# Row statistics of the FFN norm in a Mamba and FFN kernel: from VectorE's batch-norm instructions to ScalarE's accumulator output

## The chip, the cores and the metric

The kernel runs on one core of a Trainium2 chip. A core has five engines that run their own instruction streams and meet at semaphores: PE (TensorE, matrix products into PSUM), ACT (ScalarE, functions with a scale and a bias), DVE (VectorE, elementwise work and scans), POOL (GpSimd, elementwise work on SBUF) and SP (SyncE, which here issues all transfers). SBUF is the working memory with 128 partitions, PSUM holds the results of PE. The metric is the device time of one execution in microseconds (us); lower is better.

## The reference

The input `x` is 4 sequences of 2048 rows with 256 columns. One layer adds a Mamba block and then a feed-forward network (FFN), each behind a norm over the 256 columns of a row:

```
x = x + mamba(layernorm(x))        # mamba has its own norm, its own residual
x = x + ffn(layernorm(x))          # eps = 1e-5

def layernorm(x): m = mean(x, -1); v = var(x, -1); return (x - m) / sqrt(v + eps)

# mamba, inner width 512, 64 states for each inner channel:
xi, z = split(norm(x) @ W_in);  u = silu(causal_conv4(xi) + conv_b)
dt, B, C = split(u @ W_xproj);  delta = softplus(dt @ W_dt + b_dt)
h_t = h_(t-1) * exp(delta_t * A) + (delta_t * u_t) * B_t;   y_t = sum_n h_t * C_t
out = ((y + u * D) * silu(z)) @ W_out

# ffn, hidden width 768, int weights / 127:
ffn(x) = (silu(x @ wg.T) * (x @ wu.T)) @ wd.T
```

The change concerns the mean and variance of the second norm, the one ahead of the FFN.

## The kernel before

**Tiles and the scan.** The 4 x 2048 rows are worked off in 16 tiles of 512 rows (`NT = B * NQ`, tile number `n`). In a tile the recurrence over time is done as 256 scans on DVE (line 1472), each of 128 partitions by 512 time steps. Sixteen scans make a group; a group's data lie in one of three `ring` buffers. For one group, transfers spread the input `dusc` into the ring (`ring<-dusc`), POOL multiplies the ring by B in two instructions of eight scans each (line 1578), PE builds one bank of decay exponents for each scan in PSUM (line 1461, tile `a`, four banks), ACT takes their exponential in place (line 1467), DVE scans, and PE contracts the states with C (line 1496, evacuated by ACT at line 1517, and line 1530 with line 1539). After the last contraction of a group its ring is free for the next load. Line 1451 (POOL) and line 1482 (ACT) carry the state from one tile to the next.

**The dense work.** Everything else of a tile is done beside the scans of a neighbouring tile, in the order in which the main loop lists it. Beside the scans of tile `n` run: `front(n+1)` (first norm of the next tile, residual kept in the DRAM tensor `rsum`), `back(n-1)` (gate, output projection and residual of the tile before; result stored to `rsum`), `front_a(n+1)` and `front_b(n+1)` (projections, convolution, one `silu` on ACT with two table loads, softplus), and `back_b(n-1)` (second norm and FFN, with a `silu` and two table loads of its own). There are 15 such `back` and `back_b` pairs; the last tile has its own `back_early` and `back_last`.

**Residual and reload.** `residual` (line 1105) opens a PSUM bank, has ACT copy a half of the tile, 2 x 256 columns, into it (line 1112), lets PE add the products, and has ACT copy 512 columns back to SBUF (line 1115). `back` does this for both halves, then stores the tile to `rsum`. `back_b` loads it again, calls `layer_norm` and then `normalise` (line 520, four ACT instructions of 256 columns).

**The norm.** `layer_norm` (line 446) issues for each of four blocks of 128 rows a `bn_stats` and a `bn_aggr` on DVE (lines 469 and 470; mean and variance land in a PSUM bank `lp`). ACT then forms `var + eps`, its logarithm, `exp(-0.5 ln)` and a square (lines 479, 489, 490, 491), and three small DVE instructions (lines 494, 499, 504) refine the reciprocal root `rs` and form `nm = -mean * rs`.

**The order of the work.** A planner written in Python (`Planner.run`) lays out every engine's stream before the program is built. It simulates the engines with a cost for each operation and places, engine by engine, the operation with the smallest score. Scan work ("S") is scored by the time at which it could start. Dense work ("D") and contractions ("C") also have a due step, counted in scans; ahead of it they are scored up to 170 ns worse, behind it up to 230 ns better (`SLOPE`, `LEAD`, `LAG`). `dense` spreads the due steps of a tile's dense operations from step 8 to step 244 of its 256 scans, in proportion to the summed costs in program order. On PE and ACT dense work that would delay scan work by over 300 ns is scored another 300 ns worse (`HOLD`). Buffers of one name are handed out in program order. The kernel uses eight PSUM banks, four `a` and four `ps`; dense work takes its `ps` banks in program order and only where two are free. So a cost or an operation that is changed anywhere shifts due steps and can change the order elsewhere.

Of the kernel before, what the change touches and what calls it, by code (L numbers as in the profile page):

```python
# [15 lines left out]
AF = mybir.ActivationFunctionType  # L16
# [4 lines left out]
P = 128  # L21
T = 512
DM = 256
# [3 lines left out]
EPS = 1e-5  # L27
# [29 lines left out]
TINY = 60  # L57
SWITCH = 90
PAD = 0.0
SLACK = {"DVE": 300.0, "POOL": 300.0}  # L60


# [29 lines left out]
class Planner:  # L92
# [244 lines left out]
def mamba_ffn_kernel(  # L337
# [93 lines left out]
    def halves(t):  # L431
        return [(t, 0), (t, 1)]
# [11 lines left out]

        return t[:, b // 2, b % 2 : b % 2 + 2, :].rearrange("p a c -> p (a c)")

    def layer_norm(src, blocks=range(4), twice=False):

        nb = len(blocks)
        m = 2 if twice else 1
        lp, ve, rs, nm = buf("ps"), buf("s4"), buf("s4"), buf("s4")

        def sq():
            return lp.t[:, 16 : 16 + m * nb]

        def col(b):
            return b.t[:, 0 : m * nb]

        def mv():
            return lp.t[:, 0 : 2 * nb].rearrange("p (s c) -> p s c", c=2)

        def two(v):
            return v.rearrange("p (m s) -> p m s", m=m)

        def stats(j, s):
            st = buf("bst")
            op("DVE", 326, lambda: nc.vector.bn_stats(st.t, tok(src)[:, s, :]), [(src, s // 2)], [st])
            op("DVE", 205, lambda: nc.vector.bn_aggr(mv()[:, j, :], st.t), [st], [(lp, 0, j)])  # L470

        for j, s in enumerate(blocks):
            stats(j, s)
        mk = [(lp, 0, j) for j in range(nb)]

        def var(i):
            op(
                "ACT", 180,
                lambda: nc.scalar.activation(
                    ve.t[:, i * nb : (i + 1) * nb], mv()[:, :, 1], AF.Copy,  # L480
                    bias=EPS * EPS if i else EPS, scale=1.0 + EPS if i else 1.0,
                ),
                mk, [(ve, i)],
            )
# [17 lines left out]
        op(  # L502
            "DVE", TINY,
            lambda: nc.vector.scalar_tensor_tensor(  # L504
                two(nm.t[:, 0 : m * nb]), mv()[:, None, :, 0].to_broadcast([P, m, nb]), -1.0,
                two(rs.t[:, 0 : m * nb]), ALU.mult, ALU.mult,
            ),
            mk + [rs], [nm],
        )
        return rs, nm  # L510

    def normalise(dst, src, sc, blocks=range(4), o=0, ro=None):
        rs, nm = sc
        o -= blocks[0]
        ro = o if ro is None else ro

        def one(s):
            op(
                "ACT", act(DM, ptr=2),
                lambda: nc.scalar.activation(  # L520
                    tok(dst)[:, s, :], tok(src)[:, s, :], AF.Identity,
                    bias=nm.t[:, o + s : o + s + 1], scale=rs.t[:, ro + s : ro + s + 1],
                ),
                [(src, s // 2), rs, nm], [(dst, s // 2)],
            )

        for s in blocks:
            one(s)
# [176 lines left out]

    B2, yts, heads_in = {}, {}, {}

    rest, gates, last = {}, {}, {}

    def load_x(n):  # L710
        b, q = n // NQ, n % NQ
# [392 lines left out]
            ),  # L1104
        )

    def residual(pieces, reads, x1, h):

        ps = buf("ps")
        v = lambda: tok(x1)[:, h * 2 : h * 2 + 2, :].rearrange("p s c -> p (s c)")  # L1110
        open_bank(ps)
        op("ACT", act(), lambda: nc.scalar.copy(ps.t, v()), [(x1, h), ps], [ps])
        for cost, f in pieces:
            op("PE", cost, lambda f=f: f(ps.t), reads, [ps])
        op("ACT", act(T, True), lambda: nc.scalar.copy(v(), ps.t), [ps], [(x1, h)])

    def ev_add(x1, h):
        def ev(ps):
# [13 lines left out]
    def back(n):  # L1132
        r = n % R
        b, q = n // NQ, n % NQ
        y2 = buf("w8")
        for hf in range(2):
            for rh in range(2):
                ld = [buf(("yl", "w2")[rh]) for _ in range(2)]
                for _ in gate_y(n, y2, hf, rh, ld):
                    pass  # L1140
        x1 = buf("w4")
        load(lambda: tok(x1), rsum[r], 524288, r=[("rsum", r)], w=[(x1, 0), (x1, 1)])

        for h in range(2):
            yk = [(y2, hf, h) for hf in range(2)]
            residual(
                [mm_tok_add(wout, lambda k: y2.t[:, k, :], s, k, range(4)) for s in (2 * h, 2 * h + 1) for k in range(4)],
                yk + ["wout"], x1, h,
            )
        store(rsum[r], lambda: tok(x1), 524288, halves(x1), [("rsum", r)])  # L1150

    def back_b(n):
        r = n % R
        b, q = n // NQ, n % NQ
        x1 = buf("w4")
        load(lambda: tok(x1), rsum[r], 524288, r=[("rsum", r)], w=halves(x1))
        sc = layer_norm(x1)
        xn = buf("w4")
        normalise(xn, x1, sc)
        xT = buf("w4")  # L1160

        def ev_t(c):
            def ev(ps):
                op("ACT", act(T, True), lambda: nc.scalar.copy(xT.t[:, c, :], ps.t), [ps], [(xT, c)])

            return ev

        for c in range(2):
            transposes(xn, c, ev_t(c))
        hma, hmb = buf("w8"), buf("w4")  # L1170

        def hm(k):
            return hma.t[:, k, :] if k < 4 else hmb.t[:, k - 4, :]

        hk = [(hma, k) for k in range(4)] + [(hmb, k) for k in range(2)]

        def ev_g(k):
            def ev(ps):
                op("ACT", act(T, True), lambda: nc.scalar.copy(hm(k), ps.t), [ps], [hk[k]])

            return ev

        def ev_u(k):
            def ev(ps):
                up = buf("w2")
                op("ACT", act(T, True), lambda: nc.scalar.copy(up.t, ps.t), [ps], [up])  # L1186
                op(
                    "POOL", 1230, lambda: nc.gpsimd.tensor_tensor(hm(k), hm(k), up.t, ALU.mult),  # L1188
                    [up, hk[k]], [hk[k]],
                )  # L1190

            return ev

        for k in range(6):
            project(wgu, k * P, xT, ev_g(k), [("wgu", 0, k)])

        def silu():
            nc.scalar.activation(hma.t, hma.t, AF.Silu)
            nc.scalar.activation(hmb.t, hmb.t, AF.Silu)
            nc.scalar.preload_act_table_set(EXP_LN)  # L1200

        op("ACT", 5450, silu, hk, hk).tail = -1283.0
# [448 lines left out]
```

## Time and profile before

| quantity | value |
|---|---|
| median of 3 runs | 5000.17 us (4996.33 to 5005.06) |
| profiled execution, its own time | 4990.98 us |
| its span from first to last instruction | 4989.2 us |
| granted TensorE clock | 0.98 of full speed |
| DVE busy | 4758.8 us (95%) |
| POOL busy | 4697.7 us (94%) |
| PE busy | 4475.7 us (90%) |
| ACT busy | 3973.4 us (80%) |
| one tile, from its first scan to the next one's (tile 2) | 306.4 us: DVE 295.5, POOL 294.6, ACT 249.1 busy |

The profiled execution lies 9.2 us below the median of the timed runs. Busy shares are means over the whole span; an engine that is busy 95% of the time may still do a given instruction in a moment in which nothing else waits for it. The table tells how much work an engine has, not what that work is worth. For that one looks at which wait ends last around it: in the timeline of an engine the number in brackets is the time it sat idle before an instruction, and the arrow names what ended it.

### The profile page before, as it was taken

The numbers are of one execution on the slowest core, as the hardware profiler recorded it, in microseconds if no ns is written. First come the engines' busy times: TensorE is split into PE (matmuls) and PEld (weight loads), VectorE is DVE, ScalarE is ACT, GpSimd is POOL, SyncE is SP. The second block draws the span as 40 slices with busy tenths as digits, with TensorE's granted clock in tenths as the row PEclk, the third lists the DMA queues.
The fourth block names the chain that finished last, engine by engine and source line by source line (L and its number), as shares of the span: only waits on it lengthen the run. The fifth ranks groups of instructions, "written<-read, shape, count | busy, mean of one in ns | idle before, by whom it ended". The sixth has DMA issues, their size and how long they took to land.

```text
span 4989.2 us, 115894 instructions
## 1 busy us (share of the span) xinstructions
PE 4475.7 (90%) x46955; PEld 2171.1 (44%) x46955; DVE 4758.8 (95%) x4696; ACT 3973.4 (80%) x7138; POOL 4697.7 (94%) x862
## 2 busy tenths in 40 slices
PE   7889899899988989989998989989999898899888
PEld 2434344444444444444443434434444343444435
DVE  7999999999999999999999999999999999999996
ACT  6778878788787887878878787887878878788674
POOL 6999999999999999999999999999999999999994
PEclk9999999999999999999999999999999999999999
DMA  8676676666676767767667666667767677676762
GB/s 291 236 280 269 262 281 262 259 271 254 263 289 255 273 235 271 296 260 272 250 267 278 259 253 251 271 270 273 268 261 276 234 271 290 243 277 246 266 252 85
DMA packets 306346, 1299.86 MB, mean 261 GB/s; under 512 B 33617, under 2 KB 134737, under 8 KB 174866
## 3 DMA queue, kind: packets, MB, share of 16 engines
q1 hardware_dynamic: 305810, 1292.44, 67.3%
q8 instruction: 369, 6.05, 0.5%
q14 instruction: 167, 1.37, 0.1%
HBM read 1186.94 MB, written 105.38 MB: 259 GB/s over the span
## 4 chain that ended last, share of the span: by engine, by line
PE 41%; DVE 20%; ACT 15%; issue 10%; DMA 8%; POOL 5%; DVEq 0%; SPq 0%; POOLq 0%; ACTq 0%
DVE ring L1472 19%; PE a L1461 11%; PE ps L1496 9%; ACT a L1467 7%; PE ps L545 7%; DMA ring<-dusc 4%; PE ps L1097 4%; POOL ring L1578 4%; PE ps L779 3%; DMA yl<-qd 2%; PE ps L1530 2%; PE ps L898 2%; ACT mm L1517 1%; DMA dusc<-w 1%; PE ps L846 1%
## 5 line engine op out<-in xcount | busy, mean ns | idle before, releaser
L1578 POOL TENSOR_TENSOR ring<-ring,b 128x4088 f32<-128x4088 f32 (+2 forms) x512 | 4545.0, 8920 | 177.0 <-DMA ring<-dusc 110.3
L1472 DVE TENSOR_TENSOR_SCAN ring<-a,ring 128x512 f32<-128x512 f32 x4096 | 4595.0, 1195 | 104.9 <-ACT a L1467 62.5
L1467 ACT ACTIVATE a<-a,a 128x512 f32<-128x512 f32 x4096 | 2697.0, 665 | 707.3 <-PE a L1461 678.0
L1461 PE MATMUL a<-stk,selb 128*128 128x512 bf16 x5119 | 1806.7, 388 | 417.0 <-DVE ring L1472 376.5
L1496 PE MATMUL ps<-ring,cz 128*32 128x128 f32 x32768 | 1288.6, 279 | 11.1 <-issue 6.6
L1496 PEld LDWEIGHTS ps<-ring,cz 128*32 128x32 f32 x32768 | 786.3, 109 | 756.1 <-issue 699.2
L1461 PEld LDWEIGHTS <-selb 128*128 128x128 bf16 x5119 | 474.5, 98 | 1302.5 <-issue 1223.8
L545 PE MATMUL ps<-w,wgu 128*128 128x512 f32 x720 | 378.1, 608 | 0.0
L1517 ACT COPY mm<-ps 128x512 f32<-128x512 f32 x512 | 303.7, 593 | 53.0 <-PE ps L1496 52.0
L1530 PE MATMUL ps<-mm,exs 128*32 128x128 f32 (+1 forms) x4112 | 285.5, 407 | 5.8 <-ACT mm L1517 5.7
L545 PE MATMUL ps<-w,win 128*128 128x512 f32 x512 | 264.4, 601 | 0.3 <-ACT w L744 0.3
L779 PE MATMUL ps<-xi,w 128*128 128x512 f32 x480 | 248.6, 599 | 0.0
L1530 PEld LDWEIGHTS ps<-mm,exs 128*32 128x32 f32 x4112 | 117.3, 119 | 185.6 <-ACT a L1467 82.8
L1097 PE MATMUL ps<-wd,w 128*128 128x256 f32 x720 | 195.2, 387 | 0.0
L545 PEld LDWEIGHTS ps<-w,wgu 128*128 128x128 f32 x720 | 138.5, 194 | 103.9 <-issue 50.3
L1097 PEld LDWEIGHTS ps<-wd,w 128*128 128x128 f32 x720 | 132.5, 190 | 39.1 <-issue 12.7
L898 PE MATMUL ps<-w,ident 128*128 128x512 f32 x248 | 132.7, 618 | 2.8 <-ACT w L878 1.2
L1188 POOL TENSOR_TENSOR w<-w,w 128x512 f32<-128x512 f32 x90 | 114.6, 1301 | 16.0 <-ACT w L1186 15.8
L1097 PE MATMUL ps<-wout,w 128*128 128x256 f32 x480 | 128.8, 383 | 0.0
L545 PEld LDWEIGHTS ps<-w,win 128*128 128x128 f32 x512 | 96.6, 192 | 71.9 <-issue 48.8
L1041 PE MATMUL ps<-prm,yt 128*128 128x128 f32 x512 | 83.7, 294 | 34.6 <-ACT ps L1054 34.0
L520 ACT ACTIVATE w<-w,s,s 128x256 f32<-128x256 f32 x192 | 112.2, 592 | 1.9 <-DVE s L504 0.9
(147 smaller groups left out, 2381.9 us busy)
## 6 DMA issues: line engine op xcount, KB each, us to landing
ring<-dusc SPq DMA_DIRECT2D x1023, 1024.0 KB, 8.3
stk<-dsc SPq DMA_DIRECT2D x256, 96.0 KB, 5.5
qd<-w SPq DMA_DIRECT2D x32, 512.0 KB, 5.6
szd<-w SPq DMA_DIRECT2D x32, 512.0 KB, 8.3
dusc<-w SPq DMA_DIRECT2D x63, 256.0 KB, 3.6
dsc<-pk SPq DMA_DIRECT2D x63, 256.0 KB, 3.0
rsum<-w SPq DMA_DIRECT2D x31, 512.0 KB, 3.4
w<-rsum SPq DMA_DIRECT2D x31, 512.0 KB, 7.9
```

The source lines that it names most:

```text
L545: lambda ps: nc.tensor.matmul(ps, w[:, c, o : o + P], xT.t[:, c, :], start=(c == 0), stop=(c == 1)),
L779: lambda: nc.tensor.matmul(ps.t, dg.t[:, j * P : (j + 1) * P], xi.t[:, j : j + T], start=(j == 0), stop=(j == 3)),
L898: lambda: nc.tensor.matmul(ps.t, m, t.t, start=False, stop=True, skip_group_check=True),
L1097: lambda ps: nc.tensor.matmul(ps[:, (s % 2) * DM : (s % 2 + 1) * DM], src(k)[:, s * P : (s + 1) * P], w[:, k, :], start=False, stop=(k == ...
L1188: "POOL", 1230, lambda: nc.gpsimd.tensor_tensor(hm(k), hm(k), up.t, ALU.mult),
L1461: "PE", 216, lambda: nc.tensor.matmul(a.t, selb[:, p, :], stk.t, start=True, stop=True),
L1467: lambda: nc.scalar.activation(a.t, a.t, AF.Exp, scale=a2f[:, idx : idx + 1]), [a, "a2"], [a],
L1472: nc.vector.tensor_tensor_scan(v, a.t, v, 0.0, ALU.mult, ALU.add)
L1496: nc.tensor.matmul(pm.t[cg * 32 : cg * 32 + 32, (r8 % 4) * P : (r8 % 4 + 1) * P], framed(cz, blk), ring.t[:, :, blk * 8 : blk * 8 + 8], st ...
L1517: nc.scalar.copy(mm.t[:, hb * 4 : hb * 4 + 4].rearrange("p r a t -> p (r a t)"), pm.t)
L1530: nc.tensor.matmul(ex.t[jh * 32 : jh * 32 + 32, a * 16 : b * 16], framed(exs, jh * 2 + jl), mm.t[:, a:b, :, jh * 2 + jl], start=(jl == 0), ...
L1578: e.tensor_tensor(v, v, b2.t[:, None, t0:].to_broadcast([P, m, T - t0]), ALU.mult)
```

## The change

`residual` gets a tile `sums`. Where `back` calls it, the one copy of 512 columns out of PSUM becomes two ACT copies of 256 columns, each with an accumulator output that adds up its row. `back` then calls `layer_norm(x1, sums=sums)` itself, behind the store to `rsum`. In this form the norm has no `bn_stats` and `bn_aggr`: one ACT instruction makes minus the mean out of the four sums, and four ACT instructions of 256 columns square `x - mean` (the bias is minus the mean) into the upper half of the `lp` bank and add up the row. The variance is that sum over 256. The rest of the norm (lines 479 to 504) stays and moves along from `back_b` to `back`. `back_b` loads the tile as before and normalises it with the `rs` and `nm` that `back` left. `front`, and `back_last` of the last tile, keep the DVE form. A function `sums_of` is added but not called.

```diff
+ACC = 60.0
 ...
-    def layer_norm(src, blocks=range(4), twice=False):
+    def layer_norm(src, blocks=range(4), twice=False, sums=None):
 ...
+        def spread(s):
+            op(
+                "ACT", act(DM, ptr=1) + ACC,
+                lambda: nc.scalar.activation(
+                    lp.t[:, DM : 2 * DM], tok(src)[:, s, :], AF.Square,
+                    bias=sums.t[:, 4 + s : 5 + s], accum_out=sq4.t[:, s : s + 1],
+                ),
+                [(src, s // 2), (sums, 4)], [(lp, 2), (sq4, s)],
+            )
+
+        if sums is None:
+            for j, s in enumerate(blocks):
+                stats(j, s)
+            mk = [(lp, 0, j) for j in range(nb)]
+        else:
+            op(
+                "ACT", 180,
+                lambda: nc.scalar.activation(sums.t[:, 4:8], sums.t[:, 0:4], AF.Copy, scale=-1.0 / DM),
+                [(sums, s) for s in range(4)], [(sums, 4)],
+            )
+            for s in range(4):
+                spread(s)
+            mk = [(sq4, s) for s in range(4)]
 ...
-    def residual(pieces, reads, x1, h):
+    def residual(pieces, reads, x1, h, sums=None):
 ...
-        op("ACT", act(T, True), lambda: nc.scalar.copy(v(), ps.t), [ps], [(x1, h)])
+        if sums is None:
+            op("ACT", act(T, True), lambda: nc.scalar.copy(v(), ps.t), [ps], [(x1, h)])
+            return
+
+        def one(i):
+            s = h * 2 + i
+            op(
+                "ACT", act(DM, True) + ACC,
+                lambda: nc.scalar.activation(
+                    tok(x1)[:, s, :], ps.t[:, i * DM : (i + 1) * DM], AF.Copy, accum_out=sums.t[:, s : s + 1]
+                ),
+                [ps], [(x1, h), (sums, s)],
+            )
+
+        for i in range(2):
+            one(i)
 ...
         store(rsum[r], lambda: tok(x1), 524288, halves(x1), [("rsum", r)])
+        norms[n] = layer_norm(x1, sums=sums)
 ...
         load(lambda: tok(x1), rsum[r], 524288, r=[("rsum", r)], w=halves(x1))
-        sc = layer_norm(x1)
         xn = buf("w4")
-        normalise(xn, x1, sc)
+        normalise(xn, x1, norms[n])
```

More of the change, by code (lines that the diff above doesn't have):

```diff
@@ L445, in framed, with sums_of, one @@
         return t[:, b // 2, b % 2 : b % 2 + 2, :].rearrange("p a c -> p (a c)")
-    def layer_norm(src, blocks=range(4), twice=False):
+    def sums_of(src):
+        sums = buf("s4")
+        sink = buf("ps")
+        def one(s):
+            op(
+                "ACT", act(DM) + ACC,
+                lambda: nc.scalar.activation(
+                    sink.t[:, 0:DM], tok(src)[:, s, :], AF.Copy, accum_out=sums.t[:, s : s + 1]
+                ),
+                [(src, s // 2)], [sink, (sums, s)],
+            )
+        for s in range(4):
+            one(s)
+        return sums
+    def layer_norm(src, blocks=range(4), twice=False, sums=None):
         nb = len(blocks)
         m = 2 if twice else 1
-        lp, ve, rs, nm = buf("ps"), buf("s4"), buf("s4"), buf("s4")
+        lp = buf("ps")
+        sq4 = buf("s4") if sums else None
+        ve, rs, nm = buf("s4"), buf("s4"), buf("s4")
         def sq():
@@ L470, in stats, with var_in, minus_mean @@
             op("DVE", 205, lambda: nc.vector.bn_aggr(mv()[:, j, :], st.t), [st], [(lp, 0, j)])
-        for j, s in enumerate(blocks):
-            stats(j, s)
-        mk = [(lp, 0, j) for j in range(nb)]
+        def spread(s):
[17 more added lines that the diff above has]
+            )
+            for s in range(4):
+                spread(s)
+            mk = [(sq4, s) for s in range(4)]
+        def var_in():
+            return mv()[:, :, 1] if sums is None else sq4.t[:, 0:4]
+        def minus_mean():
+            return mv()[:, None, :, 0] if sums is None else sums.t[:, None, 4:8]
         def var(i):
@@ L479, in var @@
                 lambda: nc.scalar.activation(
-                    ve.t[:, i * nb : (i + 1) * nb], mv()[:, :, 1], AF.Copy,
-                    bias=EPS * EPS if i else EPS, scale=1.0 + EPS if i else 1.0,
+                    ve.t[:, i * nb : (i + 1) * nb], var_in(), AF.Copy,
+                    bias=EPS * EPS if i else EPS, scale=(1.0 + EPS if i else 1.0) / (1 if sums is None else DM),
                 ),
@@ L504, in layer_norm @@
             lambda: nc.vector.scalar_tensor_tensor(
-                two(nm.t[:, 0 : m * nb]), mv()[:, None, :, 0].to_broadcast([P, m, nb]), -1.0,
+                two(nm.t[:, 0 : m * nb]), minus_mean().to_broadcast([P, m, nb]), 1.0 if sums else -1.0,
                 two(rs.t[:, 0 : m * nb]), ALU.mult, ALU.mult,
             ),
-            mk + [rs], [nm],
+            (mk if sums is None else [(sums, 4)]) + [rs], [nm],
         )
@@ L706, in mamba_ffn_kernel @@
     B2, yts, heads_in = {}, {}, {}
-    rest, gates, last = {}, {}, {}
+    rest, gates, norms, last = {}, {}, {}, {}
     def load_x(n):
@@ L1114, in residual @@
             op("PE", cost, lambda f=f: f(ps.t), reads, [ps])
-        op("ACT", act(T, True), lambda: nc.scalar.copy(v(), ps.t), [ps], [(x1, h)])
+        if sums is None:
[3 more added lines that the diff above has]
+            s = h * 2 + i
+            op(
+                "ACT", act(DM, True) + ACC,
+                lambda: nc.scalar.activation(
+                    tok(x1)[:, s, :], ps.t[:, i * DM : (i + 1) * DM], AF.Copy, accum_out=sums.t[:, s : s + 1]
+                ),
+                [ps], [(x1, h), (sums, s)],
+            )
+        for i in range(2):
+            one(i)
     def ev_add(x1, h):
@@ L1142, in back @@
         load(lambda: tok(x1), rsum[r], 524288, r=[("rsum", r)], w=[(x1, 0), (x1, 1)])
+        sums = buf("s4")
         for h in range(2):
@@ L1147, in back @@
                 [mm_tok_add(wout, lambda k: y2.t[:, k, :], s, k, range(4)) for s in (2 * h, 2 * h + 1) for k in range(4)],
-                yk + ["wout"], x1, h,
+                yk + ["wout"], x1, h, sums,
             )
         store(rsum[r], lambda: tok(x1), 524288, halves(x1), [("rsum", r)])
+        norms[n] = layer_norm(x1, sums=sums)
     def back_b(n):
```

## The prediction

> **What bounds the kernel now.** I read the page first. DVE and POOL are both nearly full:
>
> ```profile
> PE 4475.7 (90%) x46955; PEld 2171.1 (44%) x46955; DVE 4758.8 (95%) x4696; ACT 3973.4 (80%) x7138; POOL 4697.7 (94%) x862
> ```
>
> Next, DVE's groups by shape. The scans make up 4595 us. The statistics instructions are 128 each, of which the change removes 60 (15 tiles x 4):
>
> ```profile
> L1472 DVE TENSOR_TENSOR_SCAN ring<-a,ring 128x512 f32<-128x512 f32 x4096 | 4595.0, 1195 | 104.9 <-ACT a L1467 62.5 <-POOL ring L1451 34.5 <-POOL ring L1578 7.7
> L469 DVE BATCH_NORM_STATS2 bst<-w 128x6 f32<-128x256 f32 x128 | 45.1, 410 | 26.6 <-DMA w<-rsum 24.8 <-DMA w<-in 1.7
> ...
> L470 DVE BATCH_NORM_AGGREGATE ps<-bst 128x2 f32<-128x6 f32 x128 | 21.8, 170 | 1.3
> ```
>
> This looks like a lot to win, so the third view asks where these instructions stand. DVE's timeline in tile 2, whose first scan starts at 667.8 us:
>
> ```profile
> 779.10 11.22 DVE L1472 TENSOR_TENSOR_SCAN ring<-a,ring 128x512 f32<-128x512 f32 x10
> 792.34 1.41 DVE L469 BATCH_NORM_STATS2 bst<-w 128x6 f32<-128x256 f32 x4 [2.02 <-DMA w<-rsum]
> 794.77 20.17 DVE L1472 TENSOR_TENSOR_SCAN ring<-a,ring 128x512 f32<-128x512 f32 x18 [1.02 <-ACT a L1467]
> ```
>
> All four bn_stats stand in one hole, between the scan that ends at 790.32 and the scan that starts at 794.77. What ends the hole is ACT: behind the bn_stats DVE waits another 1.02 us for an exponential. ACT's timeline says why:
>
> ```profile
> 787.49 1.28 ACT L947 ACT_TABLE_LOAD   x1
> 788.78 1.91 ACT L947 ACTIVATE w<-w 128x2048 f32<-128x2048 f32 x1
> 790.60 1.99 ACT L949 ACTIVATE w<-w 128x1024 f32<-128x1024 f32 x2
> 792.61 1.28 ACT L950 ACT_TABLE_LOAD   x1
> 793.90 0.27 ACT L1539 COPY yt<-ps 128x128 f32<-128x128 f32 x1
> 794.07 3.05 ACT L1467 ACTIVATE a<-a,a 128x512 f32<-128x512 f32 x5
> ```
>
> The silu of `front_b` holds ACT for 6.4 us (787.49 to 793.89), longer than the four banks of finished exponentials last (4 x 1.12 us). Tiles 1 to 14 all show it: the bn_stats of `back_b` stand 123.5 to 126.2 us into the tile, in a hole of 4.2 to 5.2 us, and the scan behind them waits 0.7 to 2.1 us for ACT. The hole is as long without them.
>
> Last, the waits of DVE and of POOL:
>
> ```profile
> DVE ring L1472 <- ACT a L1467: 62.5, 36, 3.5
> DVE ring L1472 <- POOL ring L1451: 34.5, 23, 5.4
> DVE bst L469 <- DMA w<-rsum: 24.8, 14, 3.1
> ```
>
> ```profile
> POOL ring L1578 <- DMA ring<-dusc: 110.3, 47, 31.1
> ...
> POOL w L1188 <- ACT w L1186: 15.8, 9, 3.0
> ```
>
> Each of the two waits for the other: POOL for a ring that the scans have left, DVE, some 286 us into most tiles, for POOL behind the FFN's six multiplications (line 1188). POOL alone has 294.6 us of work in a tile of 306.4.
>
> **Removed from DVE.** bn_stats in the holes of tiles 1 to 14: 56 x 0.35 us, and 24.8 us of waiting for the reload. Worth nothing on the path, as ACT ends the hole; were the silu gone it would be 19.7 + 24.8 = 44.5 us. In tile 15 (no `front_b`, no silu) the four stand between scans and lengthen the scan step by 0.31 us each: 1.25 us. bn_aggr: they stand about 207 us into the tile, among scans that follow each other at 1.115 us, and overlap with them; start to start, a lone one adds 0.07 us and a pair 0.29. Tiles 1 to 14 together 6.6 us (0.43, in two of them 0.74), tile 15 0.3. Sum: 6.6 + 0.3 + 1.25 = 8.2 us.
>
> The Trainium skill, "Perfetto Trace Analysis", section Identifying the Most-Contended Engine, has the engine with the highest occupancy worked on first and takes occupancy as a fair measure for Vector. By that rule the whole DVE time would count, 60 x (0.41 + 0.17) = 34.8 us, against 8.2 by the timeline. I go by the timeline.
>
> **Added to ACT.** Rows for it:
>
> ```profile
> L1115 ACT COPY w<-ps 128x512 f32<-128x512 f32 x60 | 35.3, 589 | 6.7 <-PE ps L1097 6.7
> ...
> L1054 ACT ACTIVATE ps<-w,dd 128x256 f32<-128x256 f32 x64 | 30.3, 484 | 4.4 <-PE ps L1078 4.1
> ...
> L1277 ACT COPY w<-ps 128x256 f32<-128x256 f32 x12 | 4.0, 371 | 2.3 <-PE ps L1294 2.3
> ```
>
> Copies: 4 x 0.371 for 2 x 0.589, +0.31 us. Minus the mean: 0.17 to 0.21 (lines 479 and 489). Squares: 4 x 0.484 = 1.94 (line 1054 also reads 256 columns with a pointer operand and writes PSUM). What an accumulator output costs stands in no row: at least 0, as more work cannot make the instruction shorter; at most a small ACT instruction of its own, 0.25 (line 911). I take 0.2 (lines 479 to 491 move 4 columns in 0.17 to 0.21): 8 x 0.2 = 1.6 (0 to 2.0). Sum 4.05 us a tile, 61 us in all (36 to 67). It is hidden: between 717 and 735 us, where `back` ends, ACT is busy 13.65 of 18 us and idles 0.2 to 0.45 us before nearly every exponential for want of a free bank; four banks of lead cover a run of such pieces. Without that cover it would cost its 61 us.
>
> The Trainium skill, "ScalarE: Activation LUTs", section Rules for kernel authors, speaks against the move: adds and multiplications belong on VectorE, up to about 3x faster per element in bf16. The rows here, fp32, have 0.410 for a bn_stats against 0.484 for the nearest ACT form, 1.2x. By 3x a Square would be 1.23 us, 45 us more on ACT in all.
>
> **Moved.** (a) The load of `rsum` stays; what waits for it is no longer DVE but `normalise` on ACT. In tile 2 it lands during the silu, so 0 us; at most DVE's 24.8 us, passed on to ACT, with the exponentials queued behind. (b) On SP the store of `back` waits for four copies instead of two, about 0.3 + 4 x 0.2 = 1.1 us longer, with ring loads queued behind it. In tile 2 it was issued at 730.68 and the next load still had to wait for its own ring until 736.8; in tiles 1 to 5 that wait is 5.2 to 7.6 us. 0 us; without that cover 15 x 1.1 = 16. (c) The bank `lp` is now held at the end of `back`, ahead of `front_a`, until the small DVE instructions come due (step 57 by my sum of the planner's costs, 68 us; `back` ends at 57 to 63). `front_a` works with one bank fewer for up to 10 us. It has slack: `dsc` is done at about 205 us and wanted by ring loads from about 250 (three groups of 18 us ahead of the tile's end). 0 us; at most 5 us a tile, and the waits would be on `a` and the next tile's loads.
>
> (d) `back_b` loses its only DVE instructions. Its bn_aggr came due at step 173 of 256, 206 us, and that is where they ran (206 to 210). PE's dense products pause for it from 867.8 to 886.3 us in tile 2. Without that chain (aggregates 874, `normalise` 881 to 885) the FFN can start up to 14 us earlier, ahead of its due steps, where the planner's score no longer pushes it before scan work. POOL's waits for the up-projection's copies are 15.8 us; DVE's for POOL behind them are larger (34.5 + 7.7). Between all of the 15.8 won and as much lost, as the order there is new; I take half won, 7.9 us, because early work is scored behind POOL's multiplications.
>
> Sum: 4990.98 - 8.2 - 7.9 = 4974.9 for a profiled execution. The median of the runs lies 9.2 us above the profiled one, so 4984.
>
> **Rivals.** *It is all hidden.* POOL is the bound when the bn_aggr go: lead of POOL over DVE is 0 to 1 us at each tile's start, so 8 us less on DVE is waited for POOL. Result 4992 to 5000. For it: POOL's 94%. Against it: POOL idles 2 to 4 us some 250 us into most tiles for a ring, after the bn_aggr.
>
> *It pays in full.* 34.8 + 24.8 us, 4940. Against it: the hole ends by ACT in all 14 tiles. It needs the planner to lay the silu otherwise.
>
> *Slower: `normalise` goes in right behind the silu.* Its statistics are ready early now, its input lands during the silu, and a bank for its output is free then. Four instructions of 0.59 us, 2.37 us, would stand where ACT has no lead left, and scans wait for them: 15 x 2.37 = 35.5 us, less 8.2, so 5027. It decides from 0.55 us a tile (8.2 / 15), and is measurable from 1.2. For it: the scans wait for ACT at this place already, and in tiles 9 and 13 again 30 us later (3.5 and 2.0). Against it: the planner scores exponentials first, and the dense copies that stand there now cost no wait.
>
> **How the numbers follow.** 0.2%, 10 us, is about what a measurement of this kernel can tell from no change. Forecast, a gain of 10 to 35 us: 0.34, own range 4965 to 4990. Hidden: 0.28. In full: 0.06. Slower: 0.32; as the planner lays out every stream anew, the same kind of wait may come up in another place, and no row excludes it. Faster 0.34 + 0.06 = 0.40. The range runs from 4950, half of the full gain's cases, to 5040, the slow rival with 13 us to spare; it leaves out about 0.15.
>
> **What would show it.** Right: line 469 falls from 128 to 68 instructions, the hole 125 us into a tile stays at 4 to 5 us with nothing in it and ends by ACT; the FFN's transposes come some 14 us earlier; POOL's wait at line 1188 falls; ACT's busy time rises by 36 to 67 us. Wrong: the hole shrinks with the bn_stats (full gain), or DVE's 62.5 us of waiting for line 1467 rise by over 10 us behind the silu (slower), or DVE's waits for POOL take up all that was saved.

## The result and the profile after

The changed kernel takes 5167.14 us (median of four runs, 5160.06 to 5241.46) against 4999.86 us for the kernel before on the same chip: a ratio of 1.0332 (95% interval 1.0317 to 1.0346). It is 3.3% slower. The forecast was 4984 with a range of 4950 to 5040; the result lies 127 us above that range. The execution profiled first was the longest of the four (5241.46 us) and is left out of the ratio as a slow run, so the same kernel was profiled a second time (5168.25 us, close to the median); the lines here are from that second profile. Line numbers from here on are those of the changed kernel: the scan is L1535, its exponential L1530, POOL's multiplication L1641, the last small instruction of the norm L551 (L504 before), `normalise` L567.

The busy line of the changed kernel. DVE is at 95% as before, but of a span that is 177 us longer, and its busy time is 144 us more although 120 instructions left it:

```profile
PE 4507.0 (87%) x46869; PEld 2175.0 (42%) x46869; DVE 4902.4 (95%) x4576; ACT 4002.5 (77%) x7363; POOL 4695.3 (91%) x862
```

DVE's groups by shape (busy time, mean ns of one, idle time before them and what ended it) say which instruction that is:

```profile
L1535 DVE TENSOR_TENSOR_SCAN ring<-a,ring 128x512 f32<-128x512 f32 x4096 | 4593.3, 1191 | 145.4 <-ACT a L1530 85.2 <-issue 51.2 <-POOL ring L1514 4.5
L551 DVE SCALAR_TENSOR_TENSOR s<-s,s 128x4 f32<-128x4 f32 x15 | 172.3, 11487 | 0.0
...
L490 DVE BATCH_NORM_STATS2 bst<-w 128x6 f32<-128x256 f32 x68 | 23.7, 400 | 0.1
...
L491 DVE BATCH_NORM_AGGREGATE ps<-bst 128x2 f32<-128x6 f32 x68 | 11.3, 167 | 0.7
```

The scans are as they were and the 60 + 60 statistics instructions are gone. But the instruction that forms `nm = -mean * rs` on four columns now takes 11.5 us on average, fifteen times: 172.3 us. This execution is 172.5 us longer than the median of the kernel before beside it (4995.79). That the two agree so closely is chance, as an experiment below shows: without these stalls the time falls by 150 us, and another loss is left.

Before the change the same instruction, line 504, read:

```profile
L504 DVE SCALAR_TENSOR_TENSOR s<-ps,s 128x4 f32<-128x4 f32 x15 | 2.0, 133 | 0.0
```

The same line is used by the first norm and by the last tile's norm, where nothing was changed. The view of that one source line in the changed kernel (minimum/median/maximum of the duration in ns, first and last start) puts the two side by side:

```profile
L551 DVE SCALAR_TENSOR_TENSOR s<-ps,s x18: 128/138/166, 7.7 to 5131.8; 128x8 f32<-128x8 f32 x16, 128x2 f32<-128x2 f32 x2
L551 DVE SCALAR_TENSOR_TENSOR s<-s,s x15: 136/9410/25477, 436.6 to 4909.0; 128x4 f32<-128x4 f32 x15
```

With twice the columns and one operand in PSUM (`ps`) it takes 0.14 us; with both operands in SBUF (`s,s`) it takes anything from 0.14 to 25.5 us. The operand that moved is minus the mean. The description of the change says that lines 479 to 504 stay; line 504 does, but its input does not. The diff says so in lines that the excerpt above leaves out (shortened):

```diff
+        def minus_mean():
+            return mv()[:, None, :, 0] if sums is None else sums.t[:, None, 4:8]
...
-                two(nm.t[:, 0 : m * nb]), mv()[:, None, :, 0].to_broadcast([P, m, nb]), -1.0,
+                two(nm.t[:, 0 : m * nb]), minus_mean().to_broadcast([P, m, nb]), 1.0 if sums else -1.0,
```

`mv()` is a view of the bank `lp` in PSUM, `sums` is a tile in SBUF. What the instruction waits for shows in the timelines of DVE and of POOL around one of them, in tile 4:

```profile
1374.51 1.21 DVE L1535 TENSOR_TENSOR_SCAN ring<-a,ring 128x512 f32<-128x512 f32 x1
1375.64 23.93 DVE L551 SCALAR_TENSOR_TENSOR s<-s,s 128x4 f32<-128x4 f32 x1
1399.49 8.07 DVE L1535 TENSOR_TENSOR_SCAN ring<-a,ring 128x512 f32<-128x512 f32 x7
```

```profile
1337.72 61.82 POOL L1641 TENSOR_TENSOR ring<-ring,b 128x4096 f32<-128x4096 f32 x7
1427.06 8.93 POOL L1641 TENSOR_TENSOR ring<-ring,b 128x4096 f32<-128x4096 f32 x1 [27.51 <-PE ps L826]
```

POOL multiplies without a pause from 1337.72 to 1399.54. The small instruction starts at 1375.64 and ends at 1399.57, with POOL's last multiplication. DVE works in order, so no scan runs in these 24 us. POOL, which needs the rings that the scans leave, then stands idle for 27.5 us. Its waits have grown accordingly (waits of POOL: total us, times, longest; the first was 110.3 us before):

```profile
POOL ring L1641 <- DMA ring<-dusc: 164.2, 47, 31.3
POOL ring L1641 <- PE ps L826: 62.2, 3, 27.5
POOL ring L1641 <- PE a L1524: 56.7, 12, 17.9
```

The six tiles in which L551 takes 15 us or more last 318 to 332 us, the three in which it takes less than 1 us 305 to 307.

### The profile page after: what moved, and what is told of

Same layout as the page of the kernel before. It is cut to its first block, busy times and chain, and to the rows that moved or that the text cites. A ratio compares the mean times of both kernels' runs of the same rounds, so it can differ in the third digit from the quotient of the medians.

```text
span 5239.7 us, 115514 instructions
## 1 busy us (share of the span) xinstructions
PE 4462.2 (85%) x46554; PEld 2171.1 (41%) x46869; DVE 4975.7 (95%) x4576; ACT 4002.9 (76%) x7363; POOL 4694.6 (90%) x862
## 5 line engine op out<-in xcount | busy, mean ns | idle before, releaser
L1641 POOL TENSOR_TENSOR ring<-ring,b 128x4088 f32<-128x4088 f32 (+2 forms) x512 | 4537.7, 8891 | 418.2 <-DMA ring<-dusc 217.9
L1535 DVE TENSOR_TENSOR_SCAN ring<-a,ring 128x512 f32<-128x512 f32 x4096 | 4594.7, 1197 | 147.4 <-ACT a L1530 86.8
L1530 ACT ACTIVATE a<-a,a 128x512 f32<-128x512 f32 x4096 | 2704.5, 665 | 911.6 <-PE a L1524 852.3
L1524 PE MATMUL a<-stk,selb 128*128 128x512 bf16 x4729 | 1729.0, 390 | 641.9 <-DVE ring L1535 609.3
L1559 PE MATMUL ps<-ring,cz 128*32 128x128 f32 x32768 | 1302.3, 280 | 28.9 <-issue 4.3
L1580 ACT COPY mm<-ps 128x512 f32<-128x512 f32 x512 | 304.2, 594 | 15.8 <-PE ps L1559 15.1
L826 PE MATMUL ps<-xi,w 128*128 128x512 f32 x480 | 268.9, 644 | 2.4 <-ACT ctail L821 2.3
L551 DVE SCALAR_TENSOR_TENSOR s<-s,s 128x4 f32<-128x4 f32 x15 | 245.3, 16353 | 0.0
L826 PEld LDWEIGHTS ps<-xi,w 128*128 128x128 f32 x480 | 95.1, 205 | 302.4 <-issue 286.6
## 6 DMA issues: line engine op xcount, KB each, us to landing
szd<-w SPq DMA_DIRECT2D x32, 512.0 KB, 11.5
```

The costliest lines, as they stand in the source:

```text
L551: lambda: nc.vector.scalar_tensor_tensor(two(nm.t[:, 0 : m * nb]), minus_mean().to_broadcast([P, m, nb]), 1.0 if sums else -1.0, two(rs.t[ ...
L826: lambda: nc.tensor.matmul(ps.t, dg.t[:, j * P : (j + 1) * P], xi.t[:, j : j + T], start=(j == 0), stop=(j == 3)),
L1524: "PE", 216, lambda: nc.tensor.matmul(a.t, selb[:, p, :], stk.t, start=True, stop=True),
L1530: lambda: nc.scalar.activation(a.t, a.t, AF.Exp, scale=a2f[:, idx : idx + 1]), [a, "a2"], [a],
L1535: nc.vector.tensor_tensor_scan(v, a.t, v, 0.0, ALU.mult, ALU.add)
L1559: nc.tensor.matmul(pm.t[cg * 32 : cg * 32 + 32, (r8 % 4) * P : (r8 % 4 + 1) * P], framed(cz, blk), ring.t[:, :, blk * 8 : blk * 8 + 8], st ...
```

## Experiments

Ratios are to the kernel before, run on the same chip beside each experiment; brackets are 95% intervals. Two questions are asked. Is it the place of the operands of L551 that costs the time, or the rest of the change: the accumulator instructions on ACT, the earlier place of the norm, the new order of the planner? And, once that is known, is the change without the stall a gain, and which part of it is?

### The changed kernel a second time

No edit.

> The changed kernel once more, for a second look at the 15 executions of the last small DVE instruction. Theory A (it waits for POOL, and whether it gets in between two of POOL's instructions is left to chance): durations from 0.2 to 27 us, each ending within 0.1 us of the end of a POOL instruction, but not the same ones as in the first look; 130 to 260 us together, time 5155 to 5245. A fixed cost of the instruction would give the same durations again.

Measured: 5168.25 us, the lines shown above. The fifteen instructions sum to 172.3 us, against 245.3 us in the longer execution (5241.46 us): 73 us apart, as the two times are. In tile 6 the instruction took 26.7 us in the longer execution and 8.5 in the other, in tile 13 27.0 and 0.3. So it is not a fixed price.

### The mean back in PSUM

Minus the mean is written a second time, by a second small ACT instruction, into the bank `lp`; L551 reads it there. The rest of the code is that of the changed kernel. The planner, which counts the second instruction, lays some of the dense work out in another order; on DVE 235 of the 4576 places hold another instruction.

```diff
+            def negate():
+                nc.scalar.activation(sums.t[:, 4:8], sums.t[:, 0:4], AF.Copy, scale=-1.0 / DM)
+                nc.scalar.activation(lp.t[:, 0:4], sums.t[:, 0:4], AF.Copy, scale=-1.0 / DM)
...
-            return mv()[:, None, :, 0] if sums is None else sums.t[:, None, 4:8]
+            return mv()[:, None, :, 0] if sums is None else lp.t[:, None, 0:4]
```

> The changed kernel, but minus the mean is also written to the PSUM bank lp and the last small DVE instruction of the FFN norm reads it there, so that one of its two inputs is in PSUM, as before the change. Theory A (that instruction has both inputs in SBUF in the changed kernel and cannot run while POOL multiplies): its 15 executions fall from 245 us to about 2 us (0.14 each), and the time falls from 5167 to 4975 to 5005. Theory B (the loss comes from the new order of the work, from ScalarE's added work or from the bank that is held at the end of back): the instruction may be short, but the time stays at 5120 to 5180.

Measured: 5016.97 us (seven runs, 5010.71 to 5022.73) against 5000.16, ratio 1.0034 [1.0023, 1.0045]. There is one more ACT instruction in each of the fifteen norms, and the time is 150 us less; it stays 12 us above what theory A gave. In DVE's groups by shape:

```profile
L551 DVE SCALAR_TENSOR_TENSOR s<-ps,s 128x4 f32<-128x4 f32 x15 | 2.0, 133 | 0.0
```

Fifteen times 0.133 us, as before the change. Nine tenths of the loss go with the place of one operand of four columns; the added work on ACT and the new place of the norm stay in this kernel. As the order is not quite the same, this run alone doesn't prove it; the next two kernels change nothing in the order. What is left, 0.34%, needs a second cause.

### Before, with one more small instruction, once on two SBUF operands and once on one

The opposite test: the kernel before, with its order of work left untouched, gets one more DVE instruction of four columns behind L504 in the fifteen FFN norms. Its result is not used. In the first kernel both its operands are in SBUF, in the second one of them is in PSUM.

```diff
+            if extra:
+                nc.vector.scalar_tensor_tensor(
+                    nm.t[:, 4:8], rs.t[:, 0:4], 1.0, rs.t[:, 0:4], ALU.mult, ALU.mult,
+                )
```

```diff
+            if extra:
+                nc.vector.scalar_tensor_tensor(
+                    nm.t[:, 4:8], mv()[:, :, 0], 1.0, rs.t[:, 0:4], ALU.mult, ALU.mult,
+                )
```

> The kernel before, order of the work unchanged, with one more DVE instruction of 4 columns behind the last one of each FFN norm (15 in all), both inputs in SBUF, its result unused. Theory A: these 15 take 5 to 27 us each, 100 to 300 us together, and the time rises by 70 to 250 us, to 5070 to 5250. Theory B: 0.14 us each, the time within 10 us of 5000.

> The same as the run before it in this list, but the added instruction takes one of its inputs from PSUM. Both theories: 0.14 us each, 2 us together, the time within 10 us of 5000. If it were as slow as the one with both inputs in SBUF, the number of DVE instructions and not the place of the inputs would be at fault.

Measured: two operands in SBUF 5096.56 us (four runs), ratio 1.0190 [1.0167, 1.0214]; one in PSUM 4998.08 us (ten runs), ratio 0.9994 [0.9984, 1.0003]. The group of the added instruction in the first and in the second kernel:

```profile
L508 DVE SCALAR_TENSOR_TENSOR s<-s 128x4 f32<-128x4 f32 x15 | 97.8, 6522 | 0.0
```

```profile
L508 DVE SCALAR_TENSOR_TENSOR s<-ps,s 128x4 f32<-128x4 f32 x15 | 2.2, 149 | 0.0
```

The 97.8 us account for the loss of the first kernel (96 us between the medians). The granted TensorE clock falls along with the stalls: it is 0.968 to 0.970 in the first of these kernels and 0.978 to 0.982 in the second, though PE does the same work in both, and it was 0.964 in the second profile of the changed kernel. So the lower clock there is no cause apart from the stalls. The timelines of DVE and POOL in tile 1 of the first kernel, where the two instructions follow each other (L1475 is the scan of this kernel, L1581 POOL's multiplication):

```profile
579.69 0.13 DVE L503 SCALAR_TENSOR_TENSOR s<-ps,s 128x4 f32<-128x4 f32 x1
579.74 4.85 DVE L508 SCALAR_TENSOR_TENSOR s<-s 128x4 f32<-128x4 f32 x1
584.52 11.24 DVE L1475 TENSOR_TENSOR_SCAN ring<-a,ring 128x512 f32<-128x512 f32 x10
```

```profile
575.73 8.84 POOL L1581 TENSOR_TENSOR ring<-ring,b 128x4088 f32<-128x4088 f32 x1 [0.61 <-ACT s L489]
584.52 0.20 POOL L1454 COPY ring<-carry 128x16 f32<-128x16 f32 x1
```

The first one runs in the middle of POOL's multiplication. The second starts 0.05 us later and ends at 584.59, with that multiplication (584.57). In two of the fifteen tiles the added instruction took 0.15 us; in both POOL stood idle at that moment. This settles the first question: while POOL multiplies, this DVE instruction with both operands in SBUF does not get done, small as it is; with one operand in PSUM it does.

The Trainium skill states this: "SBUF — State Buffer", section Who interferes with whom, has a VectorE instruction with two SBUF inputs contend with a GpSimd instruction that reads SBUF. By the page's section Summary: rules for kernel authors, the one of the two that issues second is blocked until the first finishes. The runs agree that it is blocked (6.5 us on average against 0.15). By the page one would expect a wait up to the end of the multiplication at hand, by an estimate from it and the 8.93 us of a multiplication at most 8.9 us; the next experiment is about the waits that were longer.

### POOL's multiplications in halves

The changed kernel, with each of POOL's instructions of eight scans issued as two of four. What POOL multiplies is the same, in 511 more instructions and 69 us more of busy time, and the end of a POOL instruction comes twice as often.

```diff
-        e.tensor_tensor(v, v, b2.t[:, None, t0:].to_broadcast([P, m, T - t0]), ALU.mult)
+        for i in range(2 if m == 8 else 1):
+            k = m // (2 if m == 8 else 1)
+            w = v[:, i * k : (i + 1) * k]
+            e.tensor_tensor(w, w, b2.t[:, None, t0:].to_broadcast([P, k, T - t0]), ALU.mult)
```

> The changed kernel with each of POOL's multiplications of eight scans issued as two of four. Theory A1 (the DVE instruction gets in at the next end of a POOL instruction): a stall is at most 4.5 us, the 15 together under 68 us, the time 5000 to 5080, with up to 50 us more of POOL work in it (512 more instructions at about 0.1 us). Theory A2 (it gets in only where POOL stands idle): the 15 stay at 200 us or more and the time at 5150 to 5230. Theory B: the stalls are beside the point, 5150 to 5230.

Measured: 5087.44 us (four runs), ratio 1.0159 [1.0135, 1.0184]. That lies between the ranges of the two theories, and neither held as it was put.

```profile
L551 DVE SCALAR_TENSOR_TENSOR s<-s,s 128x4 f32<-128x4 f32 x15 | 104.9, 6991 | 0.0
```

Eleven of the fifteen ended with the multiplication that was running (0.6 to 3.8 us; a half takes 4.56). Four waited through three to six further ends of multiplications: 27.8, 27.5, 16.9 and 13.7 us, 85.9 of the 104.9 us. So DVE got in mostly at the first end here, in the changed kernel's second profile at six of fifteen. What decides whether it gets in at the first end is not shown by any run and stays open. What ends the longer waits can be read: in the four profiles with stalls (the changed kernel twice, this kernel, and the kernel before with two operands in SBUF) 24 waits went past their first end, and each of them ended where POOL had no multiplication to go on with at once. In 16 POOL then stood idle, in 8 its small copy (line 1514) came next. The longest take 27.1 us with whole and 27.8 us with halved multiplications. For the kernel it means that a shorter POOL instruction shortens the usual wait and does not bound the worst.

### Sums at the residual, the rest of the norm at its old place

Now the second cause. This kernel has the mean in PSUM and forms the row sums at the residual, but minus the mean, the squares and the small instructions stay in `back_b`, behind the reload, where the norm of before stood.

```diff
-        norms[n] = layer_norm(x1, sums=sums)
+        norms[n] = sums
...
         load(lambda: tok(x1), rsum[r], 524288, r=[("rsum", r)], w=halves(x1))
+        sc = layer_norm(x1, sums=norms[n])
         xn = buf("w4")
-        normalise(xn, x1, norms[n])
+        normalise(xn, x1, sc)
```

> As e1_mean_psum (minus the mean read from PSUM), but the squares and the rest of the norm stay in back_b, behind the reload, where the norm was before the change; only the row sums are formed at the residual's exit from PSUM. Theory C (the 17 us that e1_mean_psum is slower than before come from the place: normalise and the softplus behind the silu shift so that ACT waits in order for a store of dusc): ACT's wait for that store falls from 87 us to under 40, DVE's wait for exponentials from 134 us to 60 to 95, time 4985 to 5008. Theory D (they come from the work added to ACT): 5010 to 5025.

Measured: 4984.03 us (twelve runs, 4980.24 to 4994.09) against 4995.79 (23 runs), ratio 0.9979 [0.9970, 0.9987]. It is faster than both kernels. The sums are kept, the stall is gone, and the only difference to the kernel at 1.0034 is the place of the norm, with the order that the planner makes of it: that place cost 0.55%, some 27 us. ACT has as much work in both (busy 4000.2 us here, 3999.0 there), so theory D falls. Of theory C's marks DVE's wait for exponentials was missed: 102.4 us, not 60 to 95.

Its DVE timeline in tile 2, the place of the hole that the prediction read before the change (lines of this kernel are one higher, the scan is L1536):

```profile
773.95 21.25 DVE L1536 TENSOR_TENSOR_SCAN ring<-a,ring 128x512 f32<-128x512 f32 x19
799.71 15.71 DVE L1536 TENSOR_TENSOR_SCAN ring<-a,ring 128x512 f32<-128x512 f32 x14 [4.51 <-ACT a L1531]
```

The hole is still there, 4.5 us, with nothing in it, and ACT ends it. In DVE's waits this reads as a loss and is none:

```profile
DVE ring L1536 <- ACT a L1531: 102.4, 37, 4.5
DVE ring L1536 <- POOL ring L1515: 31.1, 24, 5.3
```

ACT's share was 62.5 us before; the 40 us more take the place of the 24.8 us of waiting for the reload and the 19.7 us of bn_stats that used to stand in the holes.

### Where the place of the norm loses its time: three tests

In the kernel with the mean in PSUM (ratio 1.0034) DVE's waits for ACT are longer still, and so are ACT's for a store; for comparison, the third line is ACT's wait for that store in the kernel with the norm at its old place:

```profile
DVE ring L1535 <- ACT a L1530: 133.8, 49, 6.3
```

```profile
ACT w L938 <- DMA dusc<-w: 87.2, 19, 8.2
```

```profile
ACT w L938 <- DMA dusc<-w: 19.0, 9, 5.4
```

The timelines of ACT, DVE and SP in tile 3 of the first of these show one such wait:

```profile
1132.68 0.69 ACT L1530 ACTIVATE a<-a,a 128x512 f32<-128x512 f32 x1
1139.52 0.63 ACT L938 ACTIVATE w<-w 128x512 f32<-128x512 f32 x1 [6.16 <-DMA dusc<-w]
```

```profile
1126.45 10.13 DVE L1535 TENSOR_TENSOR_SCAN ring<-a,ring 128x512 f32<-128x512 f32 x9
1140.74 3.45 DVE L1535 TENSOR_TENSOR_SCAN ring<-a,ring 128x512 f32<-128x512 f32 x3 [4.16 <-ACT a L1530]
```

```profile
1120.24 0.52 SPq L424 DMA_DIRECT2D b<-bcs  x1
...
1123.47 2.73 SPq L424 DMA_DIRECT2D ring<-dusc  x3
1126.55 0.33 SPq L427 DMA_DIRECT2D dusc<-w  x1
```

The softplus (L938) wants a `w` buffer from which a store to `dusc` is still reading. SP had been held at `b<-bcs` until 1120.24, 7 us after its last issue; the loads that had queued up there then went out in one burst. The store was issued at 1126.55 behind them, on the same queue, and landed 12.9 us later. In the eleven tiles for which the trace gives the landing of this store it took 10.2 to 13.7 us; at the same place in the kernel with the norm at its old place it took 4.8 to 9.4. ACT stands, the exponentials queue behind L938, and the scans stop for 4.2 us. Summed over tiles 1 to 14, the scans stop for 52 us at 165 to 169 us into a tile; with the norm at its old place the stops at 158 to 161 us sum to 5. Of the 47 us between them 27 show in the time; DVE's waits for POOL are 28 us shorter in the slower kernel (18.8 us against 47.1). What lies behind the stops, as the timelines have it: with the norm at the end of `back`, the silu of `front_b` starts some 127 us into the tile instead of 120, and the ring loads held on SP and the store come together.

First test: the planner is told that these stores land 6 us later. It was meant to let the planner order ACT around them. The same edit was made on the kernel before.

```diff
-                slack = PAD
+                slack = 6000.0 if o.key == "late" else PAD
...
-            store(dusc[r][h][i], lambda: w.t, 262144, [w], [("dusc", r, h, i)])
+            store(dusc[r][h][i], lambda: w.t, 262144, [w], [("dusc", r, h, i)]).key = "late" if n else None
```

> As e1_mean_psum, but the planner takes every store of dusc to land 6 us later than it did, so that it does not put the instruction that reuses the store's buffer where it would wait. Theory C: ACT's wait for that store falls from 87 us to under 30, DVE's wait for exponentials from 134 us to 60 to 95, time 4980 to 5005. Theory D: ACT's wait may fall, but the time stays at 5010 to 5030.

> The kernel before with the same 6 us on the stores of dusc, as the control of the run before it in this list. ACT waits 18 us for these stores in the kernel before, so both theories expect at most 15 us from it: 4980 to 5010. If it gained as much as e6_mean_psum_late does, the gain would say nothing on the change.

Measured: on the kernel with the mean in PSUM 5018.71 us (five runs), ratio 1.0046 [1.0033, 1.0058]; on the kernel before 4994.42 us (twelve runs), 1.0000 [0.9989, 1.0010]. Nothing was gained. The waits did not move (ACT for the store 87.6 us instead of 87.2), and the store still lands 10.1 to 13.6 us after its issue: the edit did not reach what it was aimed at. The planner adds the 6 us for the instructions that read `dusc`, and gives the store's buffer free at the store's end as it did; in the traces ACT, DVE, POOL and SP run their work in the same order as without the edit. So the two runs tell nothing about the store's part; they are second measurements of the same orders (1.0046 beside 1.0034).

Second test: the store is issued by ACT instead of SP, so that it doesn't stand behind the ring loads on SP; again on both kernels. ACT, DVE and POOL keep their order in both.

```diff
-            store(dusc[r][h][i], lambda: w.t, 262144, [w], [("dusc", r, h, i)])
+            op(
+                "SP", 262144 / WIRE,
+                lambda: (nc.scalar if n else nc.sync).dma_start(dusc[r][h][i], w.t), [w], [("dusc", r, h, i)],
+            )
```

> As e1_mean_psum, order of the work unchanged, but the stores of dusc are issued by ACT instead of SP, so that they do not stand in SP's queue behind the three or four ring loads that pile up there. Theory C2 (in e1_mean_psum the whole front work slides by 7 us, SP is held by the reload of bcs until the rings come free, the ring loads go out in one burst, and the dusc store behind them lands after 12 to 14 us instead of 5 to 7, on which ACT waits in order): ACT's wait at the instruction that reuses the store's buffer falls from 87 us to under 35, DVE's wait for exponentials from 134 us to under 100, time 4988 to 5005. Theory D (the added ACT work or the held bank costs the 17 us, the wait only takes the place of others): 5010 to 5030.

> The kernel before with the stores of dusc issued by ACT, the control of the run before it in this list: its stores land after 5 to 8 us already and ACT waits only 18 us for them, so at most 12 us are to be had: 4985 to 5010.

Measured: on the kernel with the mean in PSUM 4994.77 us (eleven runs) against 4998.14, ratio 0.9988 [0.9978, 0.9997]; on the kernel before 5015.43 us (nine runs), ratio 1.0030 [1.0020, 1.0040]. The same edit wins some 23 us (1.0034 to 0.9988) where the norm stands at the end of `back`, and loses 15 us where it doesn't. The waits of ACT and of DVE in the first of them (its scan is L1538):

```profile
ACT w L938 <- DMA dusc<-w: 63.6, 27, 4.6
```

```profile
DVE ring L1538 <- ACT a L1533: 102.0, 57, 4.6
```

The store of the burst landed 7.6 to 9.4 us after its issue instead of 10.2 to 13.7, and the stops of the scans at 163 to 185 us into tiles 1 to 14 fell from 53 us to 20. So a late store in front of L938 is the likely place of most of the 27 us. It is shown in part only: ACT's wait for the store fell to 64 us and not below the 35 that was expected, and the gain came from many shorter waits instead of a few long ones. The loss on the kernel before was not expected either; ACT's wait for the store rose there from 18.2 to 43.2 us, so issuing it on ACT isn't better by itself.

## Why the prediction was wrong

**The step that failed: the part "Moved".** It prices the reload, the store, the bank and the FFN's chain, and it lets the small DVE instructions come along at nothing. In (c) they only have a due step. Two of them did move unchanged. The third, `nm = -mean * rs`, had its mean replaced: it was read out of `lp` in PSUM and is now read out of `sums` in SBUF. The diff shown with the result says so, and the 0.13 us that this instruction took was measured on `s<-ps,s` alone. Read as "the same instruction" it costs 15 x 0.13 = 2 us; in the changed kernel's second profile it took 172 us. Putting the mean back in PSUM won 150 of the 167 us, and the two experiments on the kernel before show that the place of the operand is enough. No rival had it, not even by another name: both signs were argued from ACT and from the order of work.

**The second step that failed: (c), the place priced at 0.** The prediction gave the earlier place of the norm slack on the grounds that `dsc` is done 45 us before it is wanted. The waits that came were not on that chain. ACT works in order, and what held it, as far as the second test shows it, was a buffer of the softplus that a store still read. The earlier place cost about 27 us, against a bound of 5 us a tile (75) that was named and not weighted.

**The slower rival had the right sign, and neither the place nor the mechanism.** It has `normalise` stand behind the silu with the scans waiting for it. In the kernel with the mean in PSUM two or three of the four instructions do stand at 139 to 143 us, some six to nine us behind the end of the silu, among the exponentials, and no wait follows them; the hole at 133 to 136 us is 3.9 to 4.7 us long, no longer than the 4.3 to 4.5 with the norm at its old place. The stops come 25 us later, from the store. Its mark, 10 us more waiting of DVE for ACT, was a poor one: the fastest kernel shows 40 us more.

**What held.** The hole is ACT's and keeps its length without the bn_stats (4.5 us, empty); the rule that the prediction weighed there (the Trainium skill, "Perfetto Trace Analysis", section Identifying the Most-Contended Engine) would, by the prediction's estimate, have counted 34.8 us, and the kernel with the norm at its old place won some 10. Part (a) held too: no wait for the reload of `rsum` is left on any engine in the kernel with the mean in PSUM. The store's longer hold on SP, (b), was not tested alone. The kernel with the sums and the old place wins 0.21% [0.13, 0.30], 6.5 to 15 us, in the size of the 8.2 us counted for DVE; that these and nothing else make it was not tested alone. The price of the accumulator output, for which no row existed, was taken as 0.2 us. ACT's groups in the kernel with the mean in PSUM show it as an instruction of its own:

```profile
L496 ACT ACTIVATE ps<-w,s 128x256 f32<-128x256 f32 x60 | 29.4, 490 | 0.5
L1170 ACT ACTIVATE w<-ps 128x256 f32<-128x256 f32 x60 | 22.7, 382 | 7.8 <-PE ps L1144 7.7
L496 ACT ACTIVATION_READ_ACCUMULATOR ps<-w,s 128x1 f32 x60 | 12.5, 208 | 0.0
L1170 ACT ACTIVATION_READ_ACCUMULATOR w<-ps 128x1 f32 x60 | 12.2, 204 | 0.0
```

With minus the mean (3.5 us; its second form for PSUM, 3.0, is the experiment's) and without half of the old copies (17.7) the groups sum to 63 us, close to the 61 counted. The engine's busy time, however, rose by 26 us only (3973.4 to 3999.0), below the 36 to 67 named as a mark, while the durations of all ACT instructions sum to 72 us more (4342.3 to 4414.3): neighbours overlap, so a sum of durations is not a rise in busy time.

**(d) happened and did not pay.** In the kernel with the mean in PSUM the FFN's transposes are copied out at 196 to 213 us into tiles 1 to 7 instead of 218 to 222, POOL's 15.8 us of waiting for up-projections are gone from its list, and DVE's waits for POOL fell from 42.2 to 18.8 us. That is more than the 7.9 us expected. DVE's waits for exponentials rose from 62.5 to 133.8 us at the same time, and none of it shows in the time.

## What to carry to other kernels

When an instruction is moved or its input replaced, look where each of its operands lies afterwards: here a second operand that changed from PSUM to SBUF turned 0.13 us into 11.5 us on average, beside a POOL that was 91% busy, and nothing but the letters `s<-s,s` in place of `s<-ps,s` announced it. A price read from the trace holds for that form of operands alone, so compare forms, not names. And where work is moved ahead on an engine that executes in order, ask which buffer each instruction behind it waits for, down to the store that still reads that buffer.

## What the runs showed of the hardware

- A DVE instruction on four columns with both inputs in SBUF waits while POOL multiplies, up to 27.1 us (27.8 with halved multiplications), and ends within about 0.1 us of the end of a POOL instruction; with one input in PSUM it takes 0.13 to 0.15 us while POOL multiplies.
- Such a wait is not bounded by one POOL instruction. With multiplications of 8.9 us nine of the fifteen in the second profile were longer than one of them, with halves of 4.56 us four of fifteen. All 24 waits that went past their first end, in four profiles, ended where POOL had no multiplication to go on with at once; why DVE misses the first end is open.
- An accumulator output of ACT costs a separate instruction of 0.20 to 0.21 us.
- A store of 256 KB that SP issued within 6 us behind four ring loads of 1 MB landed 10.2 to 13.7 us after its issue (eleven tiles); behind at most three such loads in 6.5 us it took 4.8 to 9.4 (fourteen tiles of the kernel with the norm at its old place). Issued by ACT, with four such loads out on SP's queue, it took 7.6 to 9.4. The median of these stores in the kernel before is 3.6 us.
